# Summing softmax weights of two head groups in one product, and turning adjacency bits by VectorE and DRAM, in a four-layer graph network

## The chip, the cores and the metric

The kernel runs on one core of a Trainium2 chip, as one launch. The metric is the device time in microseconds (us) of that core; lower is better. The engines are named as in the profile: PE (TensorE matmul), PEld (its weight load), DVE (VectorE), ACT (ScalarE), POOL (GpSimd) and SP (SyncE, here only an issuer of DMAs).

## The reference

64 independent graphs of 256 nodes with 256 features each, and one 256 by 256 integer adjacency per graph, go through four layers, each followed by a residual sum and a layer norm. All is float32.

```python
def layer0(x, adj):                 # attention with 8 heads of 32, then a feed-forward of 1024
    allowed = (adj > 0) | (swapaxes(adj, 1, 2) > 0) | eye
    q, k, v = heads(x @ Wqkv.T + bqkv)
    attn = softmax(where(allowed, q @ k.T / sqrt(32), -inf))
    x = layernorm(x + (attn @ v) @ Wo.T + bo) * ln1_g + ln1_b
    return layernorm(x + relu(x @ W1.T + b1) @ W2.T + b2) * ln2_g + ln2_b
def layer1(x, adj): ...             # graph attention: softmax of leaky_relu(f_i + g_j), masked by adj > 0
def layer2(x, adj): ...             # the same with elu
def layer3(x, adj): ...             # two relational convolutions over adj == 1, with elu
for layer in (layer0, layer1, layer2, layer3):
    x = layernorm(x + layer(x, adj))
```

The change touches only layer 0: the softmax's sums, the mask, and where b2 is added.

## The kernel before, in words

**Order.** The kernel records every operation of all 64 graphs as an object (`op`, `pe`, `dve`, `act` inside `graph(g)`), with an engine, an estimated cost, the tiles that it reads and writes, and for PE a mode. `Plan.schedule` then simulates five engines, the DMA bus, eight DMA lanes on each issuing side and the ring of buffers of every tile name (`RINGS`), and picks for each engine the ready operation with the earliest due time (`DUE` by kind of operation, `LATER` by graph; `WORTH`, `HOLD`, `WINDOW` and others weigh mode switches and waits). The instructions are issued in that order. So each engine's order is fixed when the program is built, several graphs are in flight at once, and an instruction that waits holds all behind it on its engine. After about ten graphs the order repeats with a period of one graph.

**Layer 0.** 256 nodes are two tiles of 128 partitions (NB = 2), 256 features two blocks (KB = 2).

- `masks` (L901 to L923) makes `bits` = adj > 0 in bf16 (L906), turns them with four PE products against a unit matrix into a PSUM bank (L911, mode "bits"), and from the bank makes `gm` for the later layers (L914) and `am`, the symmetric mask with the diagonal (L915, L920).
- `projections` makes q and k with features on partitions and v with nodes on partitions (L873 is the helper line of all full products).
- `attention` (L953): per key tile kt, eight score products with 32 rows of contraction (L969, mode "row"); four of them run side by side on the array. r (0 to 3) is the head within a group, hg (0 and 1) the head group. ACT takes the exponential (L975) and DVE multiplies by `am` (L977), which gives `p[kt, r]`, 128 keys by 2 groups by 256 queries. DVE adds the two key tiles (L982, `both`). Then one block in mode "col" (`values`, L987): each product yields 32 output partitions, and four for r = 0 to 3 run side by side; such four are called a round here. For each hg there is one round against a stationary matrix of ones (L991), which puts the sum over the keys on all 32 partitions of the head, and two rounds against v (L996).
- DVE takes the reciprocal of 128 by 256 sums (L1002) and multiplies (L1003) to give `ctxT`; ACT reads the inverse once, for a check on overflow (L1005).
- `product_plus` multiplies by Wo (L873) and adds x, which already holds bo. A layer norm's statistics are DVE's (L882, L884), four small root operations POOL's (L887 to L890), and the application ACT's (L894).
- `feed_forward`: x1 is turned by DVE in 32 by 32 blocks and through DRAM (`bounced`: L824, out L827, back L832), multiplied by ln1_g and increased by b2 on DVE (`with_row`, L782), and so on.

`add_row_later` (L789, via L787) is an addition by an accumulating DMA that POOL issues; it adds bo to x, ln2_b to xr, and the last residual. Such a DMA and each root operation stand in POOL's one queue. All other DMAs are issued by SP.

Of the kernel before, what the change touches and what calls it, by code (L numbers as in the profile page):

```python
# [9 lines left out]
F32 = mybir.dt.float32  # L10
# [16 lines left out]
FIRST_TURNED = 2  # L27
# [6 lines left out]
RINGS = {"x": 3, "adj": 4, "bits": 2, "am": 2, "gm": 6, "T": 4, "qk": 2, "v": 2, "p": 12, "both": 4, "inv": 1, "ctxT": 2, "X": 8,  # L34
         "xr": 1, "hid": 1, "h": 3, "e": 3, "n": 1, "rel": 3, "hi": 2, "lo": 2, "o": 4, "blocks": 1, "turned": 1, "xT": 2, "cols": 2, "pf": 3}
DRAM = {"rows": 8, "row": 6}
SMALL = {"mv": 8, "st": 4, "rstd": 8, "r": 6, "rdeg": 4}


WORTH, HOLD, WAIT, LOCK = 20.0, 0.0, 1000000.0, -0.5  # L40
WINDOW, FIRST, TAIL = 4.0, 6, 58
LANES = 8
DUE = [
    115.11, 130.1, 87.27, 113.55, 184.78, 267.91, 127.15, 3.7, 6.4, 850.28, 907.96, 17.01, 767.99, 288.87, 535.33, 276.68, 323.52, 314.8, 295.86, 329.82,
    300.15, 372.49, 286.87, 287.98, -502.68, 591.19, 64, 190.54, 194.31, 213.9, 713.3, 602.04, 241.89, 284.25, 282.43, 286.42, 332.5, 286.53, 340.1, 391.1,
    -896.08, 82.57, 223.73, 1512.3, 652.66, -43.08, 40.01, 326.22, 390.1, 385.75, 460.35, 501.93, 1085.72, 819.32, 729.09, 1434.36, 1462.97, 1572.86, 309.27, 377.7,
    422.98, 298.61, 489.54, 349.1, 349.77, 403.91, 409.77, 1039.63, 1164.93, 1206.11, 1047.88, 1793.82, 1345.99, 941.63, 462.04, -143.68, -426.28, -563.2, -305.02, 262.4,
    -8.54, -682.53, -1425.23, -878.48, -910.48, 17.76, -1230.15, -1241.9, -450.83, -995.94, -1138.75, -609.23, -940.48, -121.13, -36.53, 517.96, -269.05, 397.54, 54.48, 413,
    377.06, 153.19, 158.68, -378.26, 790.96, -31.03, 404.99, 300.98, 1238.57, 734.43, 1000.75, 626.51, 101.96, 382.13, 45.13, 270.56, -211.2, 112.91, -26.02, 715.95,
    909.95, 879.4, 1800.2, 738.61, -248.98, -17.6, 171.18, 86.17, 653.43, -436.69, 887.7, -60.25, 1415.03, -622.37, 760.39, 726.88, -39.87, 361.21, 51.78, -354.13,  # L50
    -811.15, -996.74, -21.07, -458.08, -355, -638.8, -301.25, -345.83, 35.99, -729.94, 342.61, 978.89, 501.93, 624.52, -156.62, 34.99, -355.8, -535.26, -1056.55, -853.61,
    -309.82, -604.29, -123.96, -430.91, 250.59, -935.54, -71.5, 785.28, 299.06, 741.23, 514.78, 1612.86, 44.41, -201.89, -507.28, 48.76, -1134.8, -1513.38, -738.99, -2121.1,
    -1887.25, -2427.69, -1547.71, -1074.55, -1743.55, -801.23, -1039.08, -1445.41, -1451.37, -1811.92, -1599.65, -1352.15, -803.41, 105.4, 51.2, -2.45, 905.11, 340.42, 479.09, 446.27,
    -346.11, -241.48, -1320.8, -1184.67, 227.95, -410.93, 181.58, 411.97, 33.28, 533.62, 973.02, 416.68, 625.02, -116.64, 219.42, -238.55, -103.18, 369.86, -1126.9, -254.14,
    -62.97, -478.61, -760.52, 195.37, 133.89, -1164.69, -221.19, 309.39, -223.51, -1384.43, -912.86, -586.25, -502.37, -752.61, -194.22, -177.7, -903.8, -82.98, 212.44, 450.15,
    -20.63, 600.03, 718.67, -372.99, -463.15, -655.56, -114.2, -441.38, -98.81, -1186.92, 2.55, 33.89, -212.9, 343.42, -941.93, -141.06, 434.71, -230.33, -762.23, -500.28,
    -737.15, -1236.95, 350.32, -429.54, 392.55, 735.93, -165.46, 17.17, -406.76, -280.33, -545.61, -118.67, -562.59, -662.05, -637.17, -123.17, -299.09, -894.99, -728.14, 308.8,
    -407.46, -591.06, -1279.97, -1171.47, -1185.92, -532.14, -839.14, -1199.67, -1382.19, -1710.49, -1500.13, -823.47, -1317.15, -1651.44, -1534.52, -1542.11, -1999.83, -2099.36, -2677.74, -1674.04,
    -2031.11, -886.93, -741.03, 141.07, -201.09, -665.49, -899.61, -1034.61, -519.13, 753.8, -330.91, 224.95, -439.11, -74.6, -388.8, 150.07, 320.46, 266.34, 661.45, -131.11,
    -575.29, -614.71, -909.95, -860.38, -218.26, -502.7, 299.21, -466.82, -157.72, -96.09, 95.71, -751.12, -80.72, -711.21, -1440.05, -1626.75, -1496.54, -701.82, -2131.37, -1553.57,  # L60
    -767.95, -883.9, -451.78, -721.17, -77.66, -81.75, -876.87, -264.16, -284.81, 164.33, 500.84, 572.97, 751.67, 221.66, -573.04, -421.79, -309.92, 661.24, -78.37, 822.6,
    402.49, 814.87, 925.8, 120.82, 1121.82, 521.23, 871.11, 987.71, 661.55, 675.71, 250.34, -481.05, -752.44, -688.49, -790.45, -353.78, -477.33, -799.05, -598.48, -834.15,
    135.16, 359.04, -419.04, -153.16, -427.9, -63.74, 206.11, 144.64, -396.59, 87.54, -508.49, 33.99, 247.18, -231.56, 116.24, 559.54, 113.68, 945.19, 114.83, 632.95,
    846.63, 23.88, 241.92, -60.66, 167.66, 426.06, -250.81, -25.85, -886.96, 163.03, 213.44, 144.25, -197.06, 214.87, 469.41, 48.09, 314.49, 729.23, 840.48, 272.15,
    949.87, -274.06, 407.94, 518.88, 627.68, -253.81, -324.22, 788.98, 182.1, 73.25, -283.59, -278.9, -438.37, -351.07, -11.1, 234.91, 791.22, 267.52, -262.82, 221.58,
    -55.85, -273.21, -716.88, -232.74, -243.65, -337.37, -686.64, 243.63, -363.44, 102.34, -294.19, 157.49, -122.58, 818.8, 167.06, -139.62, 564.19, 183.5, 40.04, 561.24,
    -469.96, -301.06, 183.9, -432.22, 344.47, -19.44, 175.22, -329.23, 111.52, 31.67, 0, 12.49, 16.35, 40.7, 13.03, 29.97, 79.66, 87.72, 88.16, 92.57,
    16.9, 42.2, 63.91, 67.37, 69.2, 69.57, 64.77, 66.51, 67.73, 68.1, 54.65, 63.05, 66.15, 90.74, 93.34, 103.29, 93.94, 113.24, 100.44, 111.1,
    101.32, 106.37, 89.66, 91.55, 102.68, 90.95, 92.88, 92.14, 95.53, 92.74, 96.15, 112.62, 115.22, 115.84, 108.16, 120.58, 126.02, 128.08, 123.52, 127.74,
    128.55, 132.38, 133.45, 134.52, 135.25, 136.34, 139.84, 156.74, 162.92, 141.05, 141.83, 146.74, 158.73, 159.93, 153.03, 155.22, 160.92, 162.78, 158.68, 159.54,  # L70
    161.3, 162.04, 154.36, 156.09, 161.67, 162.41, 156.95, 157.81, 160.55, 163.15, 165.1, 168.73, 172.37, 173.1, 174.18, 178.53, 179.69, 180.41, 181.13, 184.82,
    188.33, 190.19, 190.97, 195.88, 202.19, 203.65, 203.07, 206.36, 222.82, 225.76, 209.06, 211.91, 217.09, 223.82, 225.27, 228.89, 231.63, 234.38, 242.79, 245.03,
    235.73, 243.83, 244.01, 246.19, 248.14, 251.65, 257.58, 258.36, 263.28, 272.62, 274.23, 269.16, 273.95, 276.54, 341.81, 276.37, 276.67, 281.05, 288.88, 287.58,
    292.81, 294.47, 301.47, 303.32, 303.53, 307.8, 309.41, 309.85, 304.06, 309.25, 311.17, 313.08, 313.83, 318.66, 320.01, 324.08, 327.59, 217.6, 300.09, 321.45,
    331.08, 331.85, 336.77, 350.16, 352.09, 353.9, 355.27, 348.44, 350.37, 351.98, 353.57, 356.31, 359.28, 360.19, 360.79, 357.08, 357.99, 359.21, 361.32, 361.85,
    365.25, 366.27, 367.05, 374.16, 388.51, 395.12, 397.74, 400.66, 385.92, 388.51, 398.17, 401.4, 402.41, 406.64, 404.62, 407.66, 408.19, 415.16, 418.79, 420.65,
    446.91, 460.58, 469.56, 476.66, -42.08, -71.22, 47.55, 3.95, 87.01, -47.02, 84.87, 96.85, 43.29, 49.34, 127.81, 93.06, 163.1, 82.32, 60.43, 233.39,
    93.62, 90.44, -0.5, 120.06, -23.99, 59.25, 35.15, -243.24, 80.37, 53.47, 200.92, -73.58, -7.08, 5.9, -5.15, 25.23, 43.87, 9.22, -39.39, -39.72,
    -111.42, -25.63, 15.17, 9.26, 110.12, -23.73, 207.1, 32.19, 46.32, 175.57, 73.87, -13.49, 97.45, -54.1, 63.07, 26.32, 36.13, -21.71, 254.66, 142.72,
    97.69, 92.02, 135.98, 306.53, 204.66, 18, 8.92, 47.55, 119.05, -168.79, 195.29, 2.68, 311.48, 151.91, 107.66, 214.4, 509.65, 39.08, 110.14, 228.99,  # L80
    218.6, 168.24, 162.95, 261, 207.45, 107.57, 85.27, 116.9, 164.82, 190.13, 200.94, 178.43, 163.52, 204.35, 300.87, 365.21, 103.17, 173.45, 85.86, 207.98,
# [267 lines left out]
def tile_gnn_stack(ctx: ExitStack, tc: tile.TileContext, t: dict, out: bass.AP):  # L349
# [267 lines left out]
    def main_path(plan):  # L617
# [139 lines left out]
        def graph(g):  # L757
# [117 lines left out]
            def layer_norm(y):  # L875
# [21 lines left out]
                dve(0.88, stats, [y], [mv, stat])  # L897
                op("POOL", 1.8, root, [mv], [rstd], port="waits", lag=0.15)
                act(1.0, apply, [y, rstd], [y])

            def masks(adj):  # L901


# [570 lines left out]
```

## Time and profile before

| | |
|---|---|
| time, median of 3 runs | 2740.27 us (2736.58 to 2741.49) |
| the profiled execution: time, span | 2740.2 us, 2738.3 us |
| granted PE clock, mean | 0.995 |
| PE, DVE, ACT, POOL busy | 99%, 90%, 58%, 34% |
| DMA moved | 329.91 MB, mean 120 GB/s |
| sums against ones, L991 | 80.2 us of PE in 1024 records |
| products with v, L996 | 134.0 us in 2048 records |
| bits, L911 | 25.3 us in 256 records |
| reciprocal, L1002 | 217.2 us of DVE, 128 of 1729 ns |
| sum of key tiles, L982 | 169.6 us of DVE, 256 of 669 ns |

Busy time is the union of an engine's instructions, so overlapping products count once. A float32 product has two records (two passes), an F32R or bf16 product one. The chain that ended last is followed from the last instruction backwards, each time to what released it; the chain in order of time is the same chain, cut into pieces by line. A "record" in it is one instruction of the trace.

### The profile page before, as it was taken

The numbers are of one execution on the slowest core, as the hardware profiler recorded it, in microseconds if no ns is written. First come the engines' busy times: TensorE is split into PE (matmuls) and PEld (weight loads), VectorE is DVE, ScalarE is ACT, GpSimd is POOL, SyncE is SP. The second block draws the span as 40 slices with busy tenths as digits, with TensorE's granted clock in tenths as the row PEclk, the third lists the DMA queues.
The fourth block names the chain that finished last, engine by engine and source line by source line (L and its number), as shares of the span: only waits on it lengthen the run. The fifth ranks groups of instructions, "written<-read, shape, count | busy, mean of one in ns | idle before, by whom it ended". The sixth has DMA issues, their size and how long they took to land.

```text
span 2738.3 us, 48644 instructions
## 1 busy us (share of the span) xinstructions
PE 2712.7 (99%) x15808; PEld 2115.7 (77%) x15808; DVE 2465.2 (90%) x6538; ACT 1598.4 (58%) x3830; POOL 935.5 (34%) x1747
## 2 busy tenths in 40 slices
PE   8999999999999999999999999999999999999997
PEld 6887877777787787777777877877877777778774
DVE  6789989999999999999999999999999999988977
ACT  4446555556556556556555565565565555655767
POOL 2233333334333333333333333343333333332222
PEclk8999999999999999999999999999999999999999
DMA  7345545454454454554544544544545546364211
GB/s 187 95 110 130 130 116 129 119 127 123 127 135 120 128 130 121 129 124 129 133 120 124 139 119 125 135 121 127 129 121 132 125 128 147 97 143 108 51 47 40
DMA packets 609611, 329.91 MB, mean 120 GB/s; under 512 B 391694, under 2 KB 600616, under 8 KB 609352
## 3 DMA queue, kind: packets, MB, share of 16 engines
q1 hardware_dynamic: 564984, 275.72, 36.1%
q0 software_dynamic: 44368, 51.01, 11.9%
q8 instruction: 128, 2.10, 0.3%
q14 instruction: 131, 1.07, 0.1%
HBM read 182.60 MB, written 94.23 MB: 101 GB/s over the span
## 4 chain that ended last, share of the span: by engine, by line
PE 97%; DVE 1%; DMA 1%; ACT 1%; issue 0%; SPq 0%; POOL 0%; POOLq 0%
PE bank L873 80%; PE bank L969 5%; PE bank L1155 4%; PE bank L996 4%; PE bank L991 2%; PE bank L911 1%; DMA wqkv<-in_WqkvT_dram 0%; PE bank L802 0%; DMA rows<-turned 0%; ACT turned L813 0%; DVE p L977 0%; ACT e L1170 0%; DMA T<-rows 0%; DVE inv L1002 0%; ACT X L894 0%
## 5 line engine op out<-in xcount | busy, mean ns | idle before, releaser
L887 POOL TENSOR_SCALAR rstd<-mv 128x2 f32<-128x2 f32 x384 | 148.7, 387 | 1415.1 <-DVE mv L884 469.0
L873 PE MATMUL bank<-cw,T 128*128 128x512 f32 x1024 | 469.0, 592 | 0.0
L873 PE MATMUL bank<-T,w 128*128 128x256 f32 x2048 | 466.6, 380 | 0.0
L873 PE MATMUL bank<-w,hid 128*128 128x256 f32 x2048 | 457.0, 381 | 0.0
L873 PEld LDWEIGHTS bank<-w,hid 128*128 128x128 f32 x2048 | 397.0, 196 | 43.0 <-issue 3.4
L873 PEld LDWEIGHTS bank<-T,w 128*128 128x128 f32 x2048 | 384.8, 190 | 53.8 <-issue 2.0
L975 ACT ACTIVATE p<-bank 128x512 f32<-128x512 f32 x512 | 298.8, 603 | 169.9 <-PE bank L969 169.7
L894 ACT ACTIVATE X<-X,rstd 128x256 f32<-128x256 f32 x640 | 350.0, 599 | 78.1 <-POOL rstd L890 77.3
L977 DVE TENSOR_TENSOR p<-p,am 128x512 f32<-128x512 f32 x512 | 336.6, 681 | 27.4 <-ACT p L975 22.8
L888 POOL TENSOR_TENSOR rstd<-rstd,neghalf 128x2 f32<-128x2 f32 x384 | 315.0, 820 | 32.0
L873 PEld LDWEIGHTS bank<-cw,T 128*128 128x128 f32 x1024 | 198.8, 195 | 164.5 <-issue 144.8
L1031 ACT ACTIVATE hid<-bank,col_b 128x256 f32<-128x256 f32 x512 | 212.5, 469 | 105.3 <-PE bank L873 104.1
L873 PE MATMUL bank<-h,e 128*128 128x259 f32 x1024 | 264.3, 382 | 0.0
L873 PE MATMUL bank<-gw,T 128*128 128x258 f32 x1024 | 255.1, 381 | 0.0
L873 PE MATMUL bank<-xT,wqkv 128*128 128x256 f32 x1024 | 253.7, 385 | 0.9 <-DVE xT L865 0.9
L1002 DVE RECIPROCAL inv<-bank 128x256 f32<-128x256 f32 x128 | 217.2, 1729 | 30.7 <-PE bank L996 30.5
L882 DVE BATCH_NORM_STATS2 st<-X 128x6 f32<-128x256 f32 x640 | 238.3, 414 | 2.2
L873 PEld LDWEIGHTS bank<-gw,T 128*128 128x128 f32 x1024 | 198.8, 196 | 46.3 <-issue 24.6
L873 PEld LDWEIGHTS bank<-h,e 128*128 128x128 f32 x1024 | 186.5, 190 | 46.4 <-issue 14.9
L873 PEld LDWEIGHTS bank<-xT,wqkv 128*128 128x128 f32 x1024 | 193.0, 192 | 30.6 <-issue 2.5
L1155 PE MATMUL bank<-hi,rel 128*128 128x258 f32 (+1 forms) x512 | 182.6, 364 | 0.1
L824 DVE STREAM_TRANSPOSE turned<-X 128x512 f32<-128x512 f32 x236 | 166.1, 704 | 4.6 <-ACT X L894 3.1
(147 smaller groups left out, 4676.9 us busy)
## 6 DMA issues: line engine op xcount, KB each, us to landing
rows<-turned SPq DMA_DIRECT2D x295, 256.0 KB
T<-rows SPq DMA_DIRECT2D x295, 256.0 KB
adj<-in_adj_dram SPq DMA_DIRECT2D x128, 256.0 KB
x<-in_x_dram SPq DMA_DIRECT2D x64, 256.0 KB
xr<-in_x_dram SPq DMA_DIRECT2D x64, 256.0 KB
x<-row_bo POOLq DMA_DIRECT2D x64, 256.0 KB, 4.5
xr<-row_ln_b POOLq DMA_DIRECT2D x64, 256.0 KB, 3.8
out_dram<-o SPq DMA_DIRECT2D x64, 256.0 KB
```

Of the source, the lines that this page charges most:

```text
L824: dve(0.63, lambda: nc.vector.transpose(turned().rearrange("p k (b n i) -> p (k b) i n", b=4, i=NB), xt().rearrange("p i (j c) -> p j i c" ...
L873: nc.tensor.matmul(dst, lhsT=lhs(c), rhs=rhs(c), start=(c == 0), stop=(c == n - 1))
L882: nc.vector.bn_stats(stat()[:, i, :], y()[:, i, :])
L887: nc.gpsimd.tensor_scalar(rstd()[:, 0, :], mv()[:, :, 1], 1.0, EPS, op0=ALU.mult, op1=ALU.add)
L888: nc.gpsimd.tensor_tensor(rstd()[:, 0, :], rstd()[:, 0, :], neghalf[:, 0:NB], op=ALU.pow)
L894: nc.scalar.activation(y()[:, i, :], y()[:, i, :], AF.Identity, bias=rstd()[:, 1, i : i + 1], scale=rstd()[:, 0, i : i + 1])
L969: nc.tensor.matmul(s[r]()[:, hg, :], lhsT=qk()[f, KB + hg, kt * P : (kt + 1) * P], rhs=qk()[f, hg, :], start=True, stop=True)
L975: act(0.58, lambda pr=pr, k=k, sr=s[r]: nc.scalar.activation(pr(), sr(), AF.Exp, accum_out=seen_sum[:, k : k + 1]), [s[r]], [pr])
L977: dve(0.60, lambda pr=pr, kt=kt: nc.vector.tensor_tensor(pr(), pr(), am()[:, kt, None, :].to_broadcast([P, KB, N]), op=ALU.mult), [pr, am] ...
L1002: dve(1.67, lambda hg=hg, pc=pc: nc.vector.reciprocal(inv()[:, hg, :], pc()[:, 1, :]), [pc], [(inv, hg)])
L1031: act(0.36, lambda f=f, k=k, ph=ph: nc.scalar.activation(hid()[:, f + k, :], ph()[:, k, :], AF.Relu, bias=b1[:, f + k : f + k + 1]), [ph, ...
L1155: nc.tensor.matmul(pa()[:, 0:n], lhsT=rel()[:, i, j * P : (j + 1) * P], rhs=part()[:, i, 0:n], start=(c == 0), stop=(c == len(terms) - 1))
```

## The change

- **Sums.** `p` becomes one tile per key tile (128 by 2 groups by 4 heads by 256). In graphs 2 to 61 a new tile `fold` takes the place of `both`: for head group 0, DVE adds the two key tiles on partitions 0 to 63 only, for head group 1 on partitions 64 to 127 only (four additions of 64 partitions by 512, L1023 of the new kernel). Four accumulating DMAs, issued by POOL, then add the other halves of both key tiles across partitions (L1029). One round of products with a stationary `pick` of 128 by 32 (ones in columns 0 to 15 for partitions 0 to 63, in columns 16 to 31 for the rest) then gives both groups' sums, 16 partitions each. In graphs 0, 1, 62 and 63 two stationaries `every[hg]` and four rounds do it without a fold.
- **Inverse.** DVE transposes the sums in 32 by 32 blocks, takes the reciprocal of the 16 columns that differ, transposes these back to 32 partitions each, and multiplies once for both groups. The check on ACT reads the 16 columns.
- **Bits.** From graph 4 on, `bits_bounced`: two block transposes on DVE, out to DRAM and back in 64-byte runs, both issued by SP; `gm` and `am` read SBUF instead of PSUM.
- **b2** is added to x1 by an accumulating DMA (`add_row_later`) instead of DVE.
- **Order.** Other ring sizes, weights (WORTH 20.0 to 19.5, HOLD 0.0 to 0.38, WINDOW 4.0 to 4.08) and lists `DUE` and `LATER`; the whole order differs.

```diff
-RINGS = {"x": 3, "adj": 4, ... "p": 12, "both": 4, "inv": 1, ... "pf": 3}
+RINGS = {"x": 3, "adj": 3, ... "p": 3, "fold": 1, "sums": 1, "inv": 1, ... "pf": 2, "turned_b": 1, "pt": 1}
...
+    pick = filled([P, HD], F32, "pick", 0.0)
+    every = [filled([P, HD], F32, f"every{c}", 0.0) for c in range(2)]
+    for c in range(2):
+        nc.vector.memset(every[c][:, HD // 2 * c : HD // 2 * (c + 1)], 1.0)
+        nc.vector.memset(pick[P // 2 * c : P // 2 * (c + 1), HD // 2 * c : HD // 2 * (c + 1)], 1.0)
...
+            def bits_bounced(bits):
+                turned, rows, pt = new("turned_b", [P, NB, NB, P], BF16), new("rows_b", [4, P, P], BF16), tok("pt", BF16)
+                for k in range(NB):
+                    dve(0.35, lambda k=k: nc.vector.transpose(
+                        turned()[:, k].rearrange("p h (j c) -> p j h c", j=4),
+                        bits()[:, :, k * P : (k + 1) * P].rearrange("p h (a j) -> p j h a", j=4)), [bits], [(turned, k)], "uses")
+                op("SP", 0.5, lambda: nc.sync.dma_start(rows().rearrange("m p x -> p m x"),
+                                                        turned().rearrange("p k h x -> p (k h) x")), [turned], [rows],
+                   lag=SENT, size=0.5)
+                def back():
+                    r = rows()
+                    nc.sync.dma_start(pt().rearrange("p k (m c) -> p (k m) c", c=32),
+                                      bass.AP(tensor=r.tensor, offset=r.offset, ap=[[32, P], [32 * P, 16], [1, 32]]))
+                op("SP", 0.5, back, [rows], [pt], lag=BACK, size=1.1)
+                return pt
...
-                both = [new("both", [P, KB, N]) for r in range(4)]
-                for r in range(4):
-                    dve(0.60, lambda r=r: nc.vector.tensor_tensor(both[r](), p[0, r](), p[1, r](), op=ALU.add),
-                        [p[0, r], p[1, r]], [both[r]], "uses")
+                folded, fold = FIRST_TURNED <= g < B - 2, None
+                if folded:
+                    fold, half = new("fold", [P, 4, N]), P // 2
+                    for hg in range(KB):
+                        rows = slice(half * hg, half * hg + half)
+                        for r in range(0, 4, 2):
+                            dve(0.62, lambda hg=hg, rows=rows, r=r: nc.vector.tensor_tensor(
+                                fold()[rows, r : r + 2], p[0]()[rows, hg, r : r + 2, :], p[1]()[rows, hg, r : r + 2, :], op=ALU.add),
+                                [(p[kt], r + i) for kt in range(NB) for i in range(2)], [(fold, 2 * hg + r // 2)], "uses")
+                    for kt in range(NB):
+                        for hg in range(KB):
+                            into, out_of = slice(half * hg, half * hg + half), slice(half - half * hg, P - half * hg)
+                            op("POOL", 1.3, lambda kt=kt, hg=hg, into=into, out_of=out_of: nc.gpsimd.dma_start(
+                                fold()[into], p[kt]()[out_of, hg], accum_op=ALU.add),
+                               [(fold, 2 * hg), (fold, 2 * hg + 1), *[(p[kt], r) for r in range(4)]],
+                               [(fold, 2 * hg), (fold, 2 * hg + 1)], lag=5.0, size=0.9)
...
+                    terms = [(pick, lambda r: fold()[:, r, :])] if folded else [
+                        (every[hg], lambda r, hg=hg, kt=kt: p[kt]()[:, hg, r, :]) for hg in range(KB) for kt in range(NB)]
+                    for c, (lhs, rhs) in enumerate(terms):
+                        for r in range(4):
+                            nc.tensor.matmul(ps()[32 * r : 32 * r + 32, :], lhsT=lhs, rhs=rhs(r), start=(c == 0), stop=(c == len(terms) - 1))
...
-                    dve(1.67, lambda hg=hg, pc=pc: nc.vector.reciprocal(inv()[:, hg, :], pc()[:, 1, :]), [pc], [(inv, hg)])
+                dve(0.40, lambda: nc.vector.transpose(sums(), ps()), [ps], [sums])
+                dve(0.17, lambda: nc.vector.reciprocal(compact().rearrange("p (k j) -> p k j", k=KB),
+                                                       sums().rearrange("p (j k d) -> p k j d", k=KB, d=16)[:, :, :, 0]), [sums], [compact])
+                dve(0.63, lambda: nc.vector.transpose(inv().rearrange("p k n -> p (k n)"),
+                                                      compact()[:, :, None].to_broadcast([P, KB * N // 32, 32])),
+                    [compact], [inv], "uses")
+                dve(0.62, lambda: nc.vector.tensor_tensor(ctxT(), pc(), inv(), op=ALU.mult), [pc, inv], [ctxT])
...
-                with_row(x1, b2, ALU.add, [c_b2])
+                add_row_later(x1, b2, [c_b2])
```

## The prediction, made before the changed kernel ran

> **What bounds the kernel now.** I read the page first: busy time, the slices, the chain that ended last. In the fence below the reader is to see that TensorE (PE) is busy 99% of the span and in all but the first and last slices, and that the chain is PE to 97%.
>
> ```profile
> PE 2712.7 (99%) x15808; PEld 2115.7 (77%) x15808; DVE 2465.2 (90%) x6538; ACT 1598.4 (58%) x3830; POOL 935.5 (34%) x1747
> ...
> PE   8999999999999999999999999999999999999997
> ...
> PE 97%; DVE 1%; DMA 1%; ACT 1%; issue 0%; SPq 0%; POOL 0%; POOLq 0%
> ```
>
> Then the same chain in order of time, in the middle of the run (start, duration, line, records; a float32 product is two records).
>
> ```profile
> 1009.66 7.79 PE bank L873 x36
> 1017.45 0.57 PE bank L991 x8
> 1018.02 0.86 PE bank L996 x16
> 1018.88 0.43 PE bank L991 x8
> 1019.31 0.86 PE bank L996 x16
> 1020.17 0.33 PE bank L911 x4
> 1020.50 6.97 PE bank L873 x32
> 1027.47 1.94 PE bank L969 x32
> ...
> 1059.18 0.57 PE bank L991 x8
> ```
>
> Nothing but PE stands in it, and it repeats: L991 to L991 is 1059.18 - 1017.45 = 41.73 us, one graph. Of that L991 (sums of the softmax) holds two rounds and L911 (turning the adjacency bits) one piece. The busy time over exactly one such period says how much room the others have (columns: PE, PEld, DVE, ACT, POOL, granted clock, DMA share, GB/s):
>
> ```profile
> 1000.00:1041.74 41.74, 41.74 (x245) 32.65 (x244) 38.51 (x103) 24.47 (x61) 15.28 (x27) 1.00 0.52 130
> ```
>
> PE has no idle time; DVE is at 92% (38.51 of 41.74), POOL at 37%, DMA at 52%. PE work removed here is time gained, as long as no new wait appears.
>
> **What the Trainium skill says.** "TensorE: Matmul & The Clock Gate", Part 3 on packing small matmuls: products on different column groups of the array run side by side. The trace agrees: four L991 products with 32 columns each cost 0.43 us together, about one full product (L873: 6.97 us for 16). So a round costs the same whether its 32 columns hold one sum or two halves of 16. "VectorE: DVE Perf Modes", The three transpose paths: VectorE transposes 32 by 32 blocks only; no run here shows the limit itself, but L824 is used in this way, with the blocks then put in place through DRAM. "DMA: Bandwidth & Descriptors", Rules for kernel authors: an accumulating DMA beside another access of the same bytes must wait for the earlier one's semaphore. The trace of before has no such pair. The same page, Anatomy of one DMA, gives 2.0 us + bytes/436e3, an estimate of 2.6 us for 256 KB; the accumulating DMAs here are slower, so I use theirs:
>
> ```profile
> q1 hardware_dynamic: 564984, 275.72, 36.1%
> q0 software_dynamic: 44368, 51.01, 11.9%
> ...
> x<-row_bo POOLq DMA_DIRECT2D x64, 256.0 KB, 4.5
> ...
> o<-X POOLq DMA_DIRECT2D x62, 256.0 KB, 4.6
> ```
>
> **The change part by part.**
>
> *PE, on the path.* (1) Graphs 2 to 61, 60 in all, have one round of sums instead of two. The rounds cost 0.57 and 0.43 us in the chain; the first carries the entry into column mode, which stays, so 0.43 x 60 = 25.9 us go. (2) Graphs 0, 1, 62 and 63 take four rounds instead of two: + 0.86 x 4 = 3.5 us. (3) The bits of graphs 4 to 63 leave PE. The piece is 0.33 us in the chain, but part of that is leaving column mode. From the start of the last value block to the next product it is 0.979 + 0.234 us with the turn, and 0.976 us in the 11 places without it, where the products that follow run 0.05 us longer. That makes 0.979 + 0.234 - 0.976 - 0.054 = 0.18 us; a turn alone between products is 0.22. I take 0.18: 60 x 0.18 = 11.0 us (up to 13.4). (4) In the built order row mode (the scores) is entered 83 times instead of 78; an entry is 2 x 1.076 - 1.939 = 0.213 us (two single blocks against one double): + 1.1 us. The F32R gathers are split less often, by some 13 ns a place, under 1 us, left out. Sum: - 25.9 + 3.5 - 11.0 + 1.1 = **- 32.3 us**.
>
> *DVE, beside it.* Per graph go: L982 169.6/64 = 2.65, L1002 217.2/64 = 3.39, L1003 0.71, the add of b2 (L782) 0.67, together 7.42 us. New: four folds of 512 columns on half the partitions (2.68, price of L982, since columns set it), transpose of the sums 0.43 (between L1046's 226 ns for 64 columns and L824's 704 for 512), reciprocal of 16 columns 0.25 (between 153 ns for 1 and 1729 for 256), transpose 0.70, product 0.69 (L1014), two bit transposes 0.86: 5.61 us. DVE falls to about 36.7 us a graph; worth nothing directly, since PE hides it. ACT loses some 0.4 us (the check now reads 16 columns, not 512), likewise hidden.
>
> *POOL and DMA, new.* Four accumulating DMAs fold the other halves in, one more adds b2. The issue is 0.94 us (o<-X) to 1.69 us (x<-row_bo): 4 x 0.94 + 1.3 = 5.1 us, so POOL goes to about 20.4 of 41.1 us. Bytes: (240 + 64) x 256 KB = 79.7 MB; at 11.9% for 51.01 MB this is 18.6% more DMA share. The bits go out in 256-byte and come back in 64-byte runs, 2560 packets a graph: 2% by bytes, 10% by q1's mean of 28 ns a packet; I take 4%. DMA share: 0.48 to about 0.71 (0.69 to 0.77). SP issues two more DMAs a graph; in the built order some 15 others stand between the way out and the way back, and am's last step stands well ahead of its first use, so the bounce is costed at nothing; the cover is that lead, and it lies off the path as long as SP isn't blocked.
>
> *The new wait.* Two of the four accumulating DMAs write what the first two wrote, so they wait for the landing, with POOL held. Queued behind them are the add of bo and the next layer norm's four root operations. From the first issue: lands at 4.6 us, third issue there, fourth 0.9 later, lands at 10.1 us. In the built order 49 DVE instructions stand between the last fold and the transpose of the sums, at 36.7/102 = 0.36 us each 17.6 us, less 2.6 for the PE block itself: about 15 us, so **about 5 us to spare**. The scores lie some 34.5 us of PE work ahead of the sums, against 31.1 before. The wo product follows the column block by some 5.4 us (half of the w2 products, then the scores) instead of 9.3, but its DVE chain is 2.1 us instead of 4.2. Stall costed: 0, bounds - 6 (PE idle at both ends shrinks, see below) and + 60 us per us of stall in each graph.
>
> *Ends.* PE was idle 11.1 us in the first 100 us, and 14.4 us after 2650 us. The last 75 us of PE work are ordered much as before. I take no change, bounds 8 us either way.
>
> The profiled execution took 2740.2 us (span 2738.3), within 0.1 us of the median 2740.27. Forecast: 2740.2 - 32.3 = **2708 us**.
>
> **Rivals.** (a) *The fold makes PE wait, slower.* For: two serial landings under a DMA share of 0.7, and POOL held meanwhile. Against: 5 us to spare; each landing has to grow by (5 + 0.54)/2 = 2.8 us, from 4.6 to 7.4 us, to eat the gain of 0.54 us a graph. At 7.9 us each the stall is 1.6 us: 2708 + 96 = 2804 us; at 7.5 us, 2756. (b) *Small waits, gain partly lost.* Layer norms behind a held POOL, the shorter way to wo, and slower bounces through DRAM cost 0.1 to 0.4 us a graph: 2714 to 2732, say 2722 us. For: the order leaves PE no slack of its own. Against: 2500 us (100 to 2650) without a PE wait in the trace of before, with DVE tighter than it will be. (c) *The ends shorten too:* the lighter DVE, 90% busy, frees the first and last graphs: 2696 us. (d) *The change doesn't do what it says:* ruled out by the built order, with 16 bit products left of 256 and 304 sum products where 512 were.
>
> **How the numbers follow.** Forecast 0.64, (a) 0.11, (b) 0.17, (c) 0.06, and 0.02 for (b) growing until it meets the old time. About 0.2% is what a measurement can tell from no change here (2734.8 to 2745.7). Faster: 0.64 + 0.06 + 0.15 of (b) = 0.85; same 0.04; slower 0.11. The range takes in the forecast with its ends and (b), from 2694 to 2740 us, and leaves out most of (a) and the tip of (c).
>
> **What would show it.** In the profile after: the period between column blocks is 41.1 us, with one sum round of 0.57 us before two value blocks that now follow each other, and no bit product in the middle; PE still at 99%; DMA share near 0.7; DVE near 89%. Wrong if PE shows idle time in its middle slices behind the fold's DMA (a), or behind the ctxT, T or rstd chains (b); wrong in the sum if PE stays full and the period isn't 41.1 us.

## The result, and the profile after

The changed kernel takes 2756.61 us (median of 5 runs, 2746.21 to 2762.4) against 2738.04 us for the kernel before on the same chip: a ratio of 1.0062 [1.0036, 1.0088]. It is slower by 0.6%; the forecast was 2708 us. The profiled execution took 2746.21 us, the fastest of the five, so its trace shows the loss at its smallest.

The page of the changed kernel: busy times, PE's slices, queues (packets, MB, share), the chain, and two DMAs with their time to landing.

```profile
PE 2695.8 (98%) x15152; PEld 2092.1 (76%) x15152; DVE 2360.0 (86%) x6585; ACT 1529.7 (56%) x3830; POOL 1181.0 (43%) x2051
...
PE   7999999999999999999999999999999999999997
...
q1 hardware_dynamic: 720504, 291.46, 41.1%
q0 software_dynamic: 80976, 130.72, 29.8%
...
PE 65%; DVE 17%; DMA 9%; issue 3%; ACT 3%; POOL 2%; SPq 1%; DVEq 0%; ACTq 0%; POOLq 0%
...
fold<-p POOLq DMA_DIRECT2D x240, 256.0 KB, 5.0
...
x<-row_bo POOLq DMA_DIRECT2D x64, 256.0 KB, 7.7
```

PE has 656 records fewer, as planned, and its slices still read 9 except at the two ends. The chain tells another story: PE fell from 97% of it to 65%, and DVE and DMA now hold 26%. The queue of POOL's DMAs, q0, went from 11.9% of the DMA engines' time to 29.8%. The fold lands after 5.0 us; x<-row_bo, an old DMA of the same kind, needs 7.7 us instead of 4.5.

The same chain in order of time (start, duration, piece), in a stretch where it runs off PE:

```profile
1026.20 0.71 DVE turned L839
1026.95 4.60 DMA rows<-turned
1031.57 0.72 DVE turned L839
1032.31 4.82 DMA rows<-turned
1037.15 0.71 DVE turned L839
```

L839 is the block transpose of a bounce through DRAM, and `turned` is a single buffer (its ring is 1 in both kernels). VectorE can't fill it again before the DMA out of it has ended: three transposes stand 5.4 and 5.6 us apart, the second and the third each behind a DMA of 4.6 to 4.8 us. VectorE issues in order, so everything behind L839 waits with it. Its waits over the whole run (us, times, longest) include a second one of this kind, at `pf`, a row that a DMA spreads over the partitions for the graph attention of the later layers:

```profile
DVE turned L839 <- DMA rows<-turned: 88.1, 52, 4.6
...
DVE e L1134 <- DMA pf<-row: 53.9, 42, 3.5
```

In the kernel before, these two are 1.3 and 1.8 us, once each. Not all of the difference comes from the fold's DMAs, as e1 below shows. Nowhere does PE wait for the fold itself. How VectorE's hold reaches PE is seen in the timeline of that place (start, duration, engine, line, operation; in brackets the idle time before and what ended it), VectorE first:

```profile
1028.38 0.69 DVE L1056 TENSOR_TENSOR ctxT<-bank,inv 128x512 f32<-128x512 f32 x1
1031.57 0.71 DVE L839 STREAM_TRANSPOSE turned<-X 128x512 f32<-128x512 f32 x1 [2.50 <-DMA rows<-turned]
1032.20 0.65 DVE L1067 TENSOR_TENSOR X<-bank,X 128x512 f32<-128x512 f32 x1
```

and PE:

```profile
1029.82 2.10 PE L888 MATMUL bank<-w,hid 128*128 128x256 f32 x9
1031.85 2.19 PE L1006 MATMUL bank<-qk 32*128 32x256 f32 x32
1033.97 1.99 PE L888 MATMUL bank<-wo,ctxT 128*128 128x256 f32 x8
```

VectorE stands still for 2.50 us at L839. Behind it waits L1067, which reads a PSUM bank and so frees it. The score products (L1006) fill four PSUM banks for each key tile, which makes them the likely first to lack one. This block of 32 needs 2.01 us at best and took 2.19. It shows no idle time: products that run side by side overlap, and busy time is their union, so that one late product leaves no gap. Over all 45 double and 38 single score blocks, worked out from the trace's records, the excess over the shortest is 19.0 us (23 double blocks over by more than 0.1 us), against 0.1 us in the kernel before. The group of the scores shows it too (busy us, mean ns, idle before it), in the changed kernel

```profile
L1006 PE MATMUL bank<-qk 32*128 32x256 f32 x2048 | 146.8, 394 | 7.8 <-DVE X L1067 5.9 <-ACT qk L981 1.7
```

and in the kernel before

```profile
L969 PE MATMUL bank<-qk 32*128 32x256 f32 x2048 | 132.6, 390 | 0.0
```

with the same 2048 records (134.4 us in e1, which has the changed order). So part of the stall hides in the busy count, and PE at 98% is no proof that nothing waits.

### The profile page after: what moved, and what is told of

It reads as the page before. It is cut to its first block, busy times and chain, and to the rows that moved or that the text cites. A ratio compares the mean times of both kernels' runs of the same rounds, so it can differ in the third digit from the quotient of the medians.

```text
span 2744.4 us, 48371 instructions
## 1 busy us (share of the span) xinstructions
PE 2695.8 (98%) x15152; PEld 2092.1 (76%) x15152; DVE 2360.0 (86%) x6585; ACT 1529.7 (56%) x3830; POOL 1181.0 (43%) x2051
## 3 DMA queue, kind: packets, MB, share of 16 engines
q1 hardware_dynamic: 720504, 291.46, 41.1%
q0 software_dynamic: 80976, 130.72, 29.8%
## 4 chain that ended last, share of the span: by engine, by line
PE 65%; DVE 17%; DMA 9%; issue 3%; ACT 3%; POOL 2%; SPq 1%; DVEq 0%; ACTq 0%; POOLq 0%
PE bank L888 54%; DMA rows<-turned 4%; PE bank L1006 4%; DMA pf<-row 3%; PE bank L1208 3%; PE bank L1046 3%; DVE fold L1023 2%; DVE p L1014 2%; DVE turned L839 2%; PE bank L1041 1%; DVE e L1134 1%; DVE st L897 1%; ACT X L909 1%; DVE lo L1196 1%; DVE mv L899 1%
## 5 line engine op out<-in xcount | busy, mean ns | idle before, releaser
L902 POOL TENSOR_SCALAR rstd<-mv 128x2 f32<-128x2 f32 x384 | 135.9, 354 | 1041.2 <-DVE mv L899 918.0
L888 PE MATMUL bank<-T,w 128*128 128x256 f32 x2048 | 479.9, 380 | 1.1 <-DVE rdeg L1214 0.6
L888 PE MATMUL bank<-w,hid 128*128 128x256 f32 x2048 | 466.1, 382 | 1.8 <-ACT hid L1084 1.8
L903 POOL TENSOR_TENSOR rstd<-rstd,neghalf 128x2 f32<-128x2 f32 x384 | 316.1, 823 | 32.3
L1029 POOL DMA_DIRECT2D fold<-p x240 | 204.9, 870 | 156.0 <-DMA fold<-p 65.8
L888 PE MATMUL bank<-xT,wqkv 128*128 128x256 f32 x1024 | 260.4, 383 | 1.2 <-DVE xT L880 0.8
L888 PE MATMUL bank<-h,e 128*128 128x259 f32 x1024 | 254.9, 382 | 2.6 <-ACT e L1139 0.9
L839 DVE STREAM_TRANSPOSE turned<-X 128x512 f32<-128x512 f32 x236 | 166.8, 707 | 101.8 <-DMA rows<-turned 86.9
L888 PEld LDWEIGHTS bank<-h,e 128*128 128x128 f32 x1024 | 192.1, 190 | 38.1 <-issue 2.8
L1195 ACT CAST hi<-bank 128x256 fp32r<-128x256 f32 x256 | 93.1, 364 | 220.0 <-PE bank L888 219.2
```

The source lines that it names most:

```text
L839: dve(0.63, lambda: nc.vector.transpose(turned().rearrange("p k (b n i) -> p (k b) i n", b=4, i=NB), xt().rearrange("p i (j c) -> p j i c" ...
L888: nc.tensor.matmul(dst, lhsT=lhs(c), rhs=rhs(c), start=(c == 0), stop=(c == n - 1))
L902: nc.gpsimd.tensor_scalar(rstd()[:, 0, :], mv()[:, :, 1], 1.0, EPS, op0=ALU.mult, op1=ALU.add)
L903: nc.gpsimd.tensor_tensor(rstd()[:, 0, :], rstd()[:, 0, :], neghalf[:, 0:NB], op=ALU.pow)
L1029: op("POOL", 1.3, lambda kt=kt, hg=hg, into=into, out_of=out_of: nc.gpsimd.dma_start(fold()[into], p[kt]()[out_of, hg], accum_op=ALU.add), ...
L1195: act(0.27, lambda i=i, po=po: nc.scalar.copy(hi()[:, i, 0:D], po()[:, D:]), [po], [(hi, i)])
```

## The experiments

Each kernel is the changed one with an edit, of which the main lines are shown (in part without their beginnings; `...` marks a cut within a line); the order of the rest stays as it was. Times are medians, ratios are to the kernel before on the same chip, which took 2737.5 to 2738.1 us each time. The changed kernel's five runs spread over 16 us, so a difference from its median is known to within several us only. The theories: **A**, the fold's DMAs cost the time, by POOL held at a wait (A1), by their traffic (A2) or by POOL being busy (A3); A2a is the hold of VectorE at `turned`, A2b late arrivals elsewhere, A2c the length of single packets, A2d the total time of a burst. **B**: the new order and the smaller rings cost it by themselves. **C**: the bits' small packets cost it.

**e1_no_fold_dma.** The four DMAs go; the sums then lack half of the keys, and the additions put in 1.0, so that none is zero.

```diff
-op("POOL", 1.3, lambda ...: nc.gpsimd.dma_start(fold()[into], p[kt]()[out_of, hg], accum_op=ALU.add),
+op("POOL", 1.3, lambda: None,
```

> The changed kernel in its own order, with the four accumulating fold DMAs of each graph left out (the sums then cover half of the keys; 1.0 is added so that none is zero). Theory A, the fold's DMAs are the cause (their traffic or their waits): 2703 to 2718 us, near the forecast of 2708. Theory B, the new order and smaller rings are tight by themselves: 2735 us or more, as with the DMAs.

Measured: 2715.38 us (2715.26 to 2716.42), 0.9918 [0.9901, 0.9934]. The fold's DMAs cost 2756.61 - 2715.38 = 41.2 us; without them the kernel is within 7.5 us of the forecast. Its page:

```profile
PE 2680.1 (99%) x15152; PEld 2086.8 (77%) x15152; DVE 2360.2 (87%) x6585; ACT 1521.7 (56%) x3830; POOL 983.3 (36%) x1811
...
q0 software_dynamic: 61776, 67.80, 16.6%
```

The same 15152 records need 15.7 us less PE time than in the changed kernel, and PE is idle for 33.4 us instead of 48.6: together the 30.9 us between the two spans. The score blocks are back at an excess of 0.5 us. VectorE's two waits, however, don't both go:

```profile
DVE turned L839 <- DMA rows<-turned: 52.7, 46, 2.5
DVE e L1134 <- DMA pf<-row: 0.6, 1, 0.6
```

So the rest of the change holds VectorE at `turned` for 52.7 us even without the fold's DMAs, and that costs PE next to nothing. B falls as a cause by itself; but VectorE is tighter at `turned` than it was before. The chain in the middle is again PE alone:

```profile
1014.49 0.57 PE bank L1041 x8
1015.06 1.73 PE bank L1046 x32
1016.79 3.66 PE bank L888 x16
1020.45 1.94 PE bank L1006 x32
1022.39 20.94 PE bank L888 x80
...
1055.62 0.57 PE bank L1041 x8
```

One round of sums, two value blocks that follow each other, no bits, and a period of 1055.62 - 1014.49 = 41.13 us.

**e2_bits_one_copy.** Instead of the bits' way through DRAM, one plain copy of `bits` to `pt`; the mask then isn't turned.

```diff
-op("SP", 0.5, lambda: nc.sync.dma_start(rows()..., turned()...), [turned], [rows], ...)
+op("SP", 0.5, lambda: None, [turned], [rows], ...)
-op("SP", 0.5, back, [rows], [pt], lag=BACK, size=1.1)
+op("SP", 0.5, lambda: nc.sync.dma_start(pt(), bits()), [rows], [pt], lag=BACK, size=1.1)
```

> The changed kernel with the two bit DMAs through DRAM (512 packets of 256 bytes and 2048 of 64 bytes per graph) replaced by one plain copy of bits to pt of 1 KB packets (the mask is then not turned). Theory C, the small packets and the longer SP queue are the cause: 2708 to 2725 us. Theory A: little moves, 2738 to 2756 us.

Measured: 2753.12 us (2744.55 to 2760.45), 1.0051 [1.0033, 1.0068]. 146,880 packets fewer make no difference that can be told from the spread of the changed kernel. C falls.

**e3_unchained.** The third and fourth DMA add into an unread tile, so they don't wait for the first two and POOL isn't held there; the sums lack a quarter of the keys, and 1.0 is added.

```diff
-fold()[into], p[kt]()[out_of, hg], accum_op=ALU.add),
+fold()[into].rearrange("p r n -> p (r n)")[:, 0:1000] if kt == 0 else spare[into],
+p[kt]()[out_of, hg].rearrange("p r n -> p (r n)")[:, 0:1000], accum_op=ALU.add),
```

> The changed kernel with the third and fourth accumulating DMA of each graph adding into a tile that nobody reads, so that they needn't wait for the first two; bytes and issues stay (1000 of 1024 columns; the sums lack a quarter of the keys, 1.0 is added). Theory A1, the wait of the second pair, with POOL held, is the cause: 2703 to 2722 us. Theory A2, the traffic is the cause (longer round trips of all DMAs): 2738 to 2758 us.

Measured: 2778.24 us (2774.09 to 2785.35), 1.0146 [1.0126, 1.0167]: slower by another 22 us, above the ranges of both theories. The hold of POOL at the first pair (65.8 us in the changed kernel) is gone from the trace, and nothing is gained: A1 falls, and the wait turns out to be a help. The likely reason, which no run isolates, is that it keeps the four transfers from coming in one burst. VectorE's waits:

```profile
DVE e L1137 <- DMA pf<-row: 105.7, 50, 3.8
DVE turned L840 <- DMA rows<-turned: 65.0, 50, 2.9
```

Together 170.7 us instead of 142.0, and the score blocks' excess is 41.5 us instead of 19.0. Here it is the wait at `pf` that grew, while the one at `turned` shrank.

**e4_no_b2_dma.** b2 isn't added at all; its slot stays in POOL's order.

```diff
-add_row_later(x1, b2, [c_b2])
+add_later(x1, lambda: None, [c_b2], False)
```

> The changed kernel without the accumulating DMA of b2 (b2 is not added). It is 16.8 of the 79.7 MB of new accumulating traffic. Theory A2, traffic: about a fifth of the loss of 38 to 48 us comes back, 2738 to 2749 us. Theory A1: no change, 2746 to 2762 us.

Measured: 2738.8 us (2730.87 to 2745.82), 1.0003 [0.9994, 1.0012]. This one DMA of 256 KB a graph, a fifth of the new traffic, is worth 18 us, where the other four are worth 41. The two don't add up: e1 keeps b2's DMA and still comes within 7.5 us of the forecast. It is on top of the fold's traffic that it costs so much.

**e5_plain_copies.** In the places of the four DMAs, plain copies of a constant tile, nearly as large; nothing is folded.

```diff
-fold()[into], p[kt]()[out_of, hg], accum_op=ALU.add),
+fold()[into].rearrange("p r n -> p (r n)")[:, 0:1000], source[out_of]),
```

> The changed kernel with its four fold DMAs per graph turned into plain copies of the same size, still issued by POOL at the same places and with the same waits (they copy ones, 1000 of 1024 columns, over the fold tile; the sums are then constant). Theory A2, traffic: what costs is the time that the accumulating packets hold the 16 DMA engines (390 ns per 4 KB in the trace of the changed kernel, where a plain 4 KB packet took 220); plain copies hold them about half as long, so half or more of the 41 us comes back: 2720 to 2738 us. Theory A3, POOL's issue time and its waits: no change, 2746 to 2762 us.

Measured: 2719.75 us (2718.91 to 2723.51), 0.9932 [0.9915, 0.9948]. Of the 41.2 us, 36.9 are gone, just past the low end of A2's range, though q0 still holds 26.7% of the DMA engines. So the DMA share alone doesn't explain the loss. The reason given in the expectation isn't met either: 7680 packets of 591 ns hold the engines 24% shorter than 15,360 of 391 ns, not half as long. Several things differ at once: POOL issues in 588 ns instead of 869, the transfer lands 3.35 us after that instead of 4.10, its packets are half as many, POOL waits 18.6 us for the first pair instead of 65.8, and the transfer neither reads `p` nor adds. Which of them counts isn't separated here.

**e6_pool_busy.** No transfer, but POOL works at least as long in the same places (46% busy, against 43% in the changed kernel). Nothing is folded, and 1.0 is added.

```diff
-nc.gpsimd.dma_start(fold()[into], p[kt]()[out_of, hg], accum_op=ALU.add)
+nc.gpsimd.tensor_scalar(some, some, 1.0, 0.0, op0=ALU.mult, op1=ALU.add)
+nc.gpsimd.tensor_tensor(scratch, scratch, neghalf[:, 0:NB], op=ALU.pow)
```

> The changed kernel with each of the four fold DMAs per graph replaced by two small POOL operations at the same place (a copy of two columns of fold onto themselves, which waits as the DMA did for the fold's additions, and a power of two columns, together about 1.1 us; the sums cover half of the keys, 1.0 is added). POOL stays as busy, the traffic is gone. Theory A3, POOL's time delays the layer norms behind it: 2740 us or more. Theory A2, traffic: as without the DMAs, 2713 to 2722 us.

Measured: 2714.55 us (2713.78 to 2715.56), 0.9914 [0.9898, 0.9931], the same as without the DMAs. A3 falls: it is the transfers, not POOL's time.

**e7_turned_two.** All transfers stay; the tile `turned` gets two physical buffers, in the same order of instructions.

```diff
-plan.ring(name, bufs, lambda shape, dtype, i: pools["work"].tile(shape, dtype, tag=f"{name}{i}", name=name))
+plan.ring(name, bufs, lambda shape, dtype, i: pools["work"].tile(
+    shape, dtype, tag=f"{name}{next(turn) % 2 if name == 'turned' else i}", name=name))
```

> The changed kernel with two buffers in turn under the tile turned, in the same order. VectorE then needn't wait for the last outgoing DMA of the bounce before it fills the buffer again (88 us of VectorE's idle time in the profile of the changed kernel). Theory A2a, the longer round trips cost time because VectorE is held there, in front of all its other work: 2715 to 2740 us. Theory A2b, they cost it through late arrivals (T, pf, the layer norms' inputs), and this wait only takes up slack: 2746 to 2762 us.

Measured: 2725.28 us (2723.04 to 2730.0), 0.9954 [0.9937, 0.997]. The second buffer alone takes back 31.3 of the 41.2 us, with POOL held as long as before (66.9 us), the DMA share unchanged (0.76 between 500 and 2150 us, 0.75 in the changed kernel) and the outgoing DMA still slow (3.46 us, median, from its issue to that of the DMA back; 3.70 in the changed kernel, 3.36 in e1, 2.44 before). The largest waits of VectorE:

```profile
DVE X L1070 <- PE bank L891: 107.8, 59, 6.2
DVE e L1137 <- DMA pf<-row: 59.3, 43, 3.8
DVE o L1227 <- ACT e L1226: 41.0, 55, 1.5
```

VectorE now waits for PE first, which is how it should be when PE bounds; the wait at `turned` is gone, and the one at `pf` stays. The score blocks' excess is 2.6 us. A2a carries most of the loss.

**e8_bf16_sums_b2_dve.** No fold: the sums of the two key tiles are written as bf16 and multiplied in two one-pass rounds; b2 is added by DVE. The sums have bf16's precision.

```diff
-fold, half = new("fold", [P, 4, N]), P // 2
+fold, half = new("fold", [P, KB, 4, N], BF16), P // 2
-terms = [(pick, lambda r: fold()[:, r, :])] if folded else [
+terms = [(every_b[hg], lambda r, hg=hg: fold()[:, hg, r, :]) for hg in range(KB)] if folded else [
```

> A version without the new accumulating traffic: VectorE adds the key tiles on all 128 partitions for both head groups (four additions of 128 by 512, as many as before) into bf16, PE sums them in two rounds of one-pass bf16 products, b2 is added by VectorE right after the gain; the bits stay bounced, the order stays. From the 2715 us without fold DMAs: one F32 round of 0.43 us becomes two bf16 rounds of about 0.11 us, 60 x 0.21 = 13 us less, and b2's traffic goes. Theory A2: 2693 to 2708 us. If the order is what costs: 2730 us or more.

Measured: 2701.97 us (2700.86 to 2705.04), 0.9866 [0.985, 0.9883]: faster than both kernels, and 13.4 us below e1, as priced.

**e9_fold_1kb.** The fold's rows lie apart, so each DMA moves runs of 1 KB instead of 4 KB, the bytes unchanged.

```diff
-fold, half = new("fold", [P, 4, N]), P // 2
+fold, half = new("fold", [P, 4, N + 8]), P // 2
```

> The changed kernel with 8 unused columns after each head's 256 in the fold tile, so that the four fold DMAs can't be cut into runs of 4 KB and go in runs of 1 KB; bytes, order and waits stay. By the accumulating 1 KB packets seen (108 ns, against 390 for 4 KB) the engines are held about 10% longer in total, but the packets of other DMAs get in four times as often. Theory A2c, the other DMAs are held behind single long packets during a burst: faster, 2722 to 2742 us. Theory A2d, it is the total time of the burst: 2750 to 2775 us.

Measured: 2770.52 us (2765.55 to 2780.75), 1.0131 [1.0105, 1.0158]. Shorter packets make it worse by 14 us: q0 rises to 33.4%, and VectorE's wait at `turned` to 108.0 us (POOL's issue also grows, from 870 to 1066 ns, which by e6 shouldn't matter). That speaks for A2d against A2c. "DMA: Bandwidth & Descriptors" of the Trainium skill, Queues, rings and completion order, says that a DMA engine takes turns between the queues that have work for it, a packet at a time, and that such a packet is typically some 9 to 17 descriptors; whether the profile counts the same thing as a packet isn't shown here. Slower bounces beside a busy q0 agree with that, but no run here isolates it.

**e10_fold_turned_two_b2_dve.** e7, with b2 added by DVE: the repair that keeps float32.

> A repair that keeps the fold in F32: two buffers in turn under turned, and b2 added by VectorE right after the gain. If the hold of VectorE (31 us) and b2's traffic (18 us) were independent, 2756 - 49 = 2708 us; they can't both be won in full, since the forecast without any new wait is 2708 and the ends cost about 7: 2711 to 2720 us. If b2's DMA acts through the same wait only: 2722 to 2728 us, as with two buffers alone.

Measured: 2724.95 us (2723.14 to 2728.48), 0.9956 [0.9942, 0.997], the same as e7. b2's DMA, worth 18 us with one buffer, is worth nothing with two. So it most likely acted through the same wait; but VectorE does the addition here (2399.2 us busy against 2359.5), where e4 left it out, and a small gain could hide behind that.

**e11_bf16_turned_two.** e8 with two buffers under `turned`.

> The version with bf16 sums and b2 on VectorE (2702 us), with two buffers in turn under turned. VectorE still waits 48 us for the outgoing DMA there. If those waits touch PE: 2690 to 2699 us. If, without the accumulating traffic, they only take up slack: 2700 to 2705 us, no change.

Measured: 2701.29 us (2700.45 to 2702.44), 0.9865 [0.9849, 0.9882]. Without the fold's traffic the second buffer brings nothing, though e8 still waits 47.9 us at `turned`. By these runs VectorE's wait there costs time only when it is longer than what the rest has to spare.

**e12_two_rounds_b2_dve.** e8 in float32: two rounds of sums as before the change, no fold, the rest of the change kept.

```diff
-fold, half = new("fold", [P, KB, 4, N], BF16), P // 2
+fold, half = new("fold", [P, KB, 4, N]), P // 2
-terms = [(every_b[hg], lambda r, hg=hg: fold()[:, hg, r, :]) for hg in range(KB)] if folded else [
+terms = [(every[hg], lambda r, hg=hg: fold()[:, hg, r, :]) for hg in range(KB)] if folded else [
```

> The parts of the change without the fold, in F32 and exact: key tiles added on all partitions, two rounds of sums, bits bounced, the short reciprocal, b2 on VectorE, the changed kernel's order. Two F32 rounds instead of two bf16 ones cost 60 x 2 x 0.32 = 38 us over the 2702 us of the bf16 version: 2738 to 2742 us, no better than before. If the rounds cost less than their price because PE then has slack elsewhere: 2715 to 2730 us.

Measured: 2740.53 us (2737.97 to 2742.37), 1.0008 [0.9999, 1.0017]. The rest of the change gains no time by itself in this order: the period falls from 41.75 to 41.57 us, about the bits' 0.18, but 60 times that is spent, by the prices of the forecast, on the edge graphs' rounds, the row entries and the ends. The 25.2 us from here to e1 fit the second round (25.9 forecast), though e1 also adds b2 by a DMA.

## Why the prediction was wrong

**The PE sum was right.** The forecast took 32.3 us off PE; e1's PE busy time is 2680.1 us, 32.6 less than before. The period was to be 41.1 us; between graphs 13 and 53 it is 41.15 us in e1 (mean; 41.75 before). In the changed kernel its median is 41.25 and its shortest 41.10, but the mean 41.53: most of the stall falls on some graphs, and 17 of 40 periods are over 41.3 us. (A period runs from the start of one block of sums to the next.)

**Loads and landings were right.** DMA share forecast 0.71 (0.69 to 0.77), seen 0.75. VectorE forecast 36.7 us a graph, seen 37.1 in e1 (1487.66 us over 1650, times 41.15). POOL forecast 20.4 us, seen 19.1 (759.21 over 1650, times 41.53). The fold's additions on half of the partitions take 682 ns each, about L982's 669, as priced. The bits were given 4% of DMA share; with one copy in their place q1 falls by 3.6 points, and it was right that they cost nothing in time. The fold's DMAs were to land after 4.6 us each; they land after 5.0. All four take 12.0 us (median, first issue to last landing) instead of 10.1, and the last lands 4.5 us ahead of the sums (median; 0.9 at the least), so PE never waits for it. Rival (a) did not happen: that it names 2756 us, the measured time, for landings of 7.5 us is chance. One reading was wrong, with nothing in the sum resting on it: the trace of before does have accumulating DMAs beside another access of the same bytes. POOL waits there 27.3 us, in six waits at L787, for loads of `xr`, to which it then adds.

**The step that failed is "Stall costed: 0".** It looked at the one wait that the change adds, the fold's own chain, and found it covered. It didn't ask what the new traffic does to the transfers already there, nor how much work of VectorE is left between two fills of a buffer that they drain. The fold's DMAs cost 41.2 us, 0.69 us in each of 60 graphs (e1), and 31.3 us of that came through the hold of VectorE at `turned` (e7). Two things meet there. The first is the order: between 529 and 2150 us, at least ten other VectorE instructions stand between two transposes into `turned` in the kernel before (6.0 us with the transpose itself); in the changed kernel one pair in each graph has only four, the new chain of the inverse (2.8 us), which is the first pair of the chain shown above. Ahead of the second transposes of these 38 pairs VectorE idles 65.3 us in all (45.2 in e1, none in e7). The other is the traffic: the time from the issue of a bounce's DMA out (rows<-turned) to the issue of the DMA back, in the same stretch, is 2.44 us before, 3.36 in e1 and 3.70 in the changed kernel (medians; 90th percentiles 3.52, 5.68 and 6.88). So a large part of the slower trips, too, comes with the rest of the change, without costing PE time in e1; what the fold's DMAs add on top did. No run put the old order beside the new traffic, so the order's part is read from the traces alone.

Rival (b) named "slower bounces through DRAM" and priced them, with two other waits, at 0.1 to 0.4 us a graph: mechanism named, price too low. Its counterargument, that no PE wait had been seen "with DVE tighter than it will be", was the wrong comparison. VectorE did get lighter (86% busy against 90%); what mattered is that it issues in order and fills a single buffer, drained by a DMA, 295 times in 64 graphs.

**"About 5 us to spare" was the wrong slack.** The slack that counted was `turned`'s: from one transpose to the next. The close pair was there to be seen in the built order, and a DMA of 4.6 us held its second transpose by 2.50 us.

**The ends** were given no change, with 8 us either way. Without the fold the kernel misses 2707.9 by 7.5 us while its PE sum came true, so idle time grew: 33.4 us in e1, 25.6 before. 4.0 us of this is PE's wait for the first weights, 7.8 us in e1 against 3.8, two waits each. The chain at the start of the kernel before is

```profile
4.71 12.04 DMA wqkv<-in_WqkvT_dram
16.79 5.84 PE bank L873 x14
```

and of the changed kernel

```profile
4.20 16.33 DMA wqkv<-in_WqkvT_dram
```

The weights arrive at 20.53 us (19.87 in e1) instead of 16.75, although their last DMA is issued earlier, at 4.20 us instead of 4.71: it takes longer to land. SP's DMAs around it differ in the two orders, and no run changed them, so the cause stays open. Where the other 4 us lie wasn't followed up. The size was within the bound, at its wrong end.

**What would show it.** The text named idle time in PE's middle slices as the sign of failure. Between 500 and 2150 us it is only 4.81 of 1650 us (columns as in the prediction's table of one period):

```profile
500.00:2150.00 1650.00, 1645.19 (x9215) 1283.40 (x9213) 1474.33 (x4089) 909.28 (x2332) 759.21 (x1270) 1.00 0.75 164
```

The chain shares and the period would have been the better test; the digits can't show a stall of 1%, half of which is counted as busy.

**What stays open.** With two buffers some 10 us of the fold's cost remain (2725.28 against 2715.38). VectorE's 59.3 us of waits at `pf` are the likeliest place: it has two buffers, three before the change, and no run gave the third back. SP, too, issues in order, and it waits for the DMAs out of `turned` 500.1 us there, against 429.4 in e1; what that holds up wasn't separated. Why plain copies of nearly the same size cost 37 us less than accumulating ones isn't settled either.

## What to carry to other kernels

When a change adds DMA traffic, list the single-buffered tiles that a DMA drains and an in-order engine refills, see how much other work the engine has between two fills, and ask what happens if each of those DMAs takes twice as long; the new transfer's own landing is only half the question. A second buffer at that place (31 us here) can be worth as much as the change itself. A bounding engine that runs several small products side by side can lose time without showing idle: compare the busy time of the same records before and after.

## What the runs showed of the hardware

- Accumulating DMAs were dear beside plain ones on the same queue: 391 ns (mean) for a packet of 4 KB, 108 ns for 1 KB in the changed kernel, where e5's plain packets of 8000 bytes took 591 ns, some 23% less a byte than those of 4 KB; and POOL's issue took 869 ns against 588.
- Four of them without a wait between the pairs (e3, 2778 us) cost more than four in two pairs, the second behind the first (2757 us). The wait was worth 22 us.
- 122,880 packets of 64 bytes took 11 ns each, and taking them away (e2) brought no time that could be told from the spread.
- Two rounds of bf16 sums, with one record a product instead of two, take 0.33 us in the chain of e11, with the entry into column mode, where one float32 round takes 0.57 us.
- A block transpose of VectorE, a reciprocal of 16 columns and a block transpose back (419, 250 and 707 ns) replaced two reciprocals of 1729 ns.
